# A two-layer LoRA residual kernel: W1's first rows turned by TensorE, two operand sums moved to adding DMAs, and G transposed by VectorE

## The chip, the cores and the metric

The kernel runs on one core of a Trainium2 chip. The metric is the device time of one execution in microseconds (us). The engines are TensorE (PE: matmuls; PEld: its weight loads), VectorE (DVE), ScalarE (ACT), GpSimd (POOL) and SyncE (SP). DMAs are issued from the queues of SP, ACT and POOL and move data on 16 DMA engines. Everything is float32.

## The reference

Two residual layers, each with a LoRA adapter that a token of the sequence selects:

```
# x: (8, 256, 1024); W0, W1: (1024, 1024); ranks 32 (layer 0) and 16 (layer 1)
x = x + x @ W0.T + 0.5 * (x @ A0[i0[b]]) @ B0.T
x = x + x @ W1.T + bias + 2 * (x @ A1[i1[b]]) @ B1[i1[b]]
```

Here `i0[b]` and `i1[b]` pick one of 3 and one of 24 (A1 and B1 hold 32) for each of the 8 sequences b.

## The kernel before, in words

**What is computed.** The kernel adds the identity to both weights and multiplies the two layers into one matrix, M = (W0 + I)^T (W1 + I)^T, then sends every sequence through M. The LoRA terms and the bias become a product of rank 64 per sequence that is added to the same sums. All large products are Strassen-Winograd products of 2x2 blocks (7 products and a handful of block sums), on two levels.

**Tiles.** `w0n` holds W0 + I, `w1T` holds the transposed W1 + I, `tw` its block sums; later the same space holds parts of M and of its sums. `m11`, `m21`, `m22` hold parts of M. `units` is 8 pieces of 128x1024: first W1 as it lands, later the sequences, landed and transposed. `s_all` is 4 pieces of 128x1024: the four sums s[0] to s[3] of the left operand that is being multiplied. `work` holds what was taken out of PSUM. The 8 PSUM banks are used in two sets of four: X and Y.

**Stages, as PE goes through them.**

- Start: 15 warm-up matmuls of `ident` by itself (L945), then 32 matmuls `first` (L978; 4 groups, 4 chunks k, 2 column halves) for the first block product. For each k, DVE transposes W1's first rows in 32x32 blocks (`turn_w1`, L227), adds the identity to their diagonal (L235) and to W0's (`diag_w0`, L182). SP loads W1's first half-block in four DMAs of 512-byte runs (`load_w1`, L168), then W0 (`load_w0`, L176), then the second half-block.
- The rest of the first block product as an inner Strassen product (`Second`, L530), then the LoRA products `prepare_up` (L723), `prepare_down` (L750) and `prepare_cross` (L764). `prepare_down` makes G^T = A1^T (W0 + I) for the 8 sequences, 128x1024, and ACT copies it to `gT`, a part of `work`.
- `product6` of the first group (L288, at 51.7 us), then `finish_down`: 8 PE transposes of `gT` (L778), copied from PSUM to `g1` by ACT (L779). `fill_down` (POOL, L817) later copies a sequence's 16 columns of `g1` into its `down`. Then the other block products (L288) and the last two row tiles of M as inner Strassen products (`Chain`, L530).
- Four pairs of sequences (`for q in range(B // 2)`). Each pair takes 7 inner Strassen products (`product`, L530), alternately into X and Y; in between come the down product of the next pair (`low_start`, L788, and `low_end`, L806) and the updates of rank 64 (L530 and L550).

**What sets the order.** The schedule is manual: each engine and each queue runs its instructions in the order in which the program writes them, and waits for semaphores. So the place of a line in the program is its place in its engine's queue.

**The lines that the steps below touch.** In the chain: `form` (L604 to L610) turns the seven products of a bank set into four blocks; the last one before the pairs, `form(chain.keep5, X, ...)`, comes after an ACT copy of slot 1 (L1135). `sums_1` to `sums_4` (L838, L841, L844, L847) make s[0] to s[3] of a pair on DVE, 128x1024 each; `z_sums` (L489) makes the four inner sums of one such operand. `Operand.sums` (L424 to L427) and `sums_rest` (L439) make the block sums of the right operand on DVE; `sums_dma` (L433 on ACT, L435 on POOL) makes three of them as ACT copies with a sign and POOL DMAs that add. `turn_x` (L240) transposes a landed sequence on DVE; `load_x` (L153) lands it in 8 SP DMAs of 64 KB. `add_up` (L515) adds a PSUM set to `work`, `keep` (L511, ACT) copies it there. `end` (L863) writes the last blocks.

In the first pair DVE makes, in this order: z of s[0], the sums of ops "t2", s[1] (L841), z of s[1], `diff`, chain t4, s[3] (L847), a rest sum (L439), z of s[3], s[2] (L844), the transposes of the next pair.

Of the kernel before, what the change touches and what calls it, by code (L numbers as in the profile page):

```python
# [10 lines left out]
ALU = mybir.AluOpType  # L11
# [9 lines left out]
P = 128  # L21
NH = 512
L0_SCALING = 16 / 32
L1_SCALING = 32 / 16
MLOW = 64
BIAS = 48
NWARM = 15
NV7 = 7
NWORK = 3
NUNIT = 8  # L30
NV = 2
NU = 2
NLOW = 4
NQ = NH // 2
NB = 4
# [6 lines left out]
def kernel(  # L42
# [120 lines left out]
    def load_w1(wq, h: int, i: int, lo: int = 0, hi: int = NR):  # L163

        rows = slice(h * NH + lo * SQ, h * NH + hi * SQ)
        for g in range(NG):
            cols = slice(i * NH + g * P, i * NH + (g + 1) * P)
            nc.sync.dma_start(  # L168
                wq[g * SQ : (g + 1) * SQ, lo:hi, :],
                w1[rows, cols].rearrange("(t q) c -> q t c", q=SQ),  # L170
            )

    def load_w0(k: int, i: int):
        cols = slice(i * NH, (i + 1) * NH)
        rows = w0[(k // NB) * NH : (k // NB + 1) * NH, cols]
        nc.sync.dma_start(  # L176
            w0n[:, k, cols], rows.rearrange("(p m) c -> p m c", m=NB)[:, k % NB, :]
        )

    def diag_w0(k: int):  # L180
        diag = w0n[:, k].rearrange("p (i q m) -> p i m q", i=2, m=NB)[:, k // NB, k % NB]
        nc.vector.tensor_tensor(diag, diag, ident, ALU.add)  # L182
# [66 lines left out]
    def new_bank():  # L249
        ring.append(ring.pop(0))  # L250
        return ring[-1]

    def low_bank():

        while ring[0] not in sets[0]:
            new_bank()
        return new_bank()

# [254 lines left out]
    def add_up(v, ps):  # L513
        for n in (3, 2, 1, 0):
            nc.vector.tensor_tensor(at_home(v, n), whole(ps, n), at_home(v, n), ALU.add)  # L515

    def low_region(ps):
        return ps[3][:, NQ:NH]
# [240 lines left out]
    def prepare_cross():  # L759
# [11 lines left out]
        nc.scalar.copy(cross.rearrange("p b r -> p (b r)"), pe)  # L771

    def finish_down():
        for h in range(NO):
            pt = (banks[7] if h else low_bank()).rearrange("p (m q) -> p m q", m=NB)
            chunks = gT[h].rearrange("p (j q c) -> p j c q", q=P, c=NX)
            for m in range(NB):
                nc.tensor.transpose(pt[:, m, :], chunks[:, m // NX, m % NX], ident)  # L778
            nc.scalar.copy(  # L779
                g1[:, NB * h : NB * (h + 1)].rearrange("p k b r -> p k (b r)"), pt  # L780
            )

# [33 lines left out]
    def fill_down(b: int):  # L816
        nc.gpsimd.tensor_copy(downs[b % NV][:, :, R0:RR], g1[:, :, b, :])  # L817

    class Pair:
# [26 lines left out]
        def sums_4(self):  # L846
            nc.vector.tensor_tensor(self.s[:, 3], self.x["12"], self.s[:, 1], ALU.subtract)  # L847

        def diff(self):
# [72 lines left out]
    with tc.manual_schedule(engines=ORDERED):  # L922
# [3 lines left out]
        wq[0, 0] = new_w1(0, 0)  # L926
        for n in range(2):
            load_w1(wq[0, 0], 0, 0, n * mid, (n + 1) * mid)
            if n == 0:
                for k in range(NB):  # L930
                    load_w0(k, 0)
        wq[0, 1] = new_w1(0, 1)
# [9 lines left out]

        for n in range(NWARM):
            bank, i = banks[4 + n // 4], n % 4
            nc.tensor.matmul(  # L945
                bank[:, i * P : (i + 1) * P],
                ident,
                ident,
                start=(i == 0),
                stop=True,  # L950
                skip_group_check=True,
            )
        raw0, raw1 = load_indices(idx0, 0), load_indices(idx1, 1)
# [22 lines left out]
        def first(g, k: int, n: int):  # L976
# [8 lines left out]
            )  # L985

        for k in range(NB):
            turn_w1(wq[0, 0], 0, k, 0, mid)
            diag_w0(k)
            for g in w_groups:  # L990
                first(g, k, 0)
# [61 lines left out]
        bias_rows(0)  # L1053
        load_up(0)
        for i, which in enumerate(("21", "22")):
            raws[which] = load_x(1, i, 6 + i)
# [10 lines left out]
        one.product6()  # L1067
        finish_down()
        seconds[1].form()
# [42 lines left out]
        for which in ("21", "22"):  # L1112
# [4 lines left out]
        chain.product(Y, "s4", "22", False)  # L1117
        ops["22"].sums_dma()
        ops["11"].sums_rest()
        add_up(chain.m12, Y)  # L1120
# [9 lines left out]
            low=(  # L1130
                lambda: low_start(0, pair.x, low_pl),
                lambda: low_end(0, low_pl),
            ),
        )
        nc.scalar.copy(chain.keep5[:, SLOT[1] * NQ : (SLOT[1] + 1) * NQ], slot(X, 1))  # L1135
        form(chain.keep5, X, chain.block(m21))
# [3 lines left out]
        ops["t3"].sums_dma()  # L1140
        z_sums(pair.sq(0), z_early[1])
        ops["t2"].sums()
        pair.sums_2()
        pending = []
# [7 lines left out]
        for q in range(B // 2):  # L1152
# [33 lines left out]
            if early:  # L1186
                chain.sums_m("t4")
                pair.sums_4()

# [9 lines left out]
            z_sums(pair.sq(3), pair.z[3])  # L1199
            if early:  # L1200
                pair.sums_3()
            if more:
# [40 lines left out]
            if not more:  # L1243
# [13 lines left out]
                low=(  # L1257
                    lambda: low_start(q + 1, following.x, pl7),
                    lambda: low_end(q + 1, pl7),
                ),  # L1260
            )
            nc.scalar.copy(kept2[:, SLOT[1] * NQ : (SLOT[1] + 1) * NQ], slot(X, 1))
            form(kept1)
# [53 lines left out]
```

## Time and profile before

| | us |
|---|---|
| median of three runs (329.24 to 329.58) | 329.51 |
| the profiled execution, its own time | 328.95 |
| its span in the trace | 327.2 |
| PE busy | 320.3 |
| DVE busy | 258.1 |
| ACT, POOL busy | 58.0, 65.6 |
| first L978 matmul starts | 7.13 |
| last matmul's chain ends, the tail follows | 323.9 |

The difference of 1.75 us between the profiled execution's time and its span lies outside what the trace records. In the lines of the profile, "x30" counts records; a float32 matmul of this kernel leaves two records, so 15 warm-up matmuls are x30 and 32 `first` matmuls are x64. In the timeline a line begins with start and length of a merged group; its bracket gives the idle time of the engine before it and what ended it. In the chain and wait views, "A <- B" reads: A waited for B. The `MATMUL` ends are modelled and overlap, so distances between starts are what counts. No PE wait is longer than 1.5 us, and between 32 and 130 us the trace shows none.

### The profile page before, as it was taken

The numbers are of one execution on the slowest core, as the hardware profiler recorded it, in microseconds if no ns is written. First come the engines' busy times: TensorE is split into PE (matmuls) and PEld (weight loads), VectorE is DVE, ScalarE is ACT, GpSimd is POOL, SyncE is SP. The second block draws the span as 40 slices with busy tenths as digits, with TensorE's granted clock in tenths as the row PEclk, the third lists the DMA queues.
The fourth block names the chain that finished last, engine by engine and source line by source line (L and its number), as shares of the span: only waits on it lengthen the run. The fifth ranks groups of instructions, "written<-read, shape, count | busy, mean of one in ns | idle before, by whom it ended". The sixth has DMA issues, their size and how long they took to land.

```text
span 327.2 us, 4443 instructions
## 1 busy us (share of the span) xinstructions
PE 320.3 (98%) x1506; PEld 248.8 (76%) x1506; DVE 258.1 (79%) x494; ACT 58.0 (18%) x124; POOL 65.6 (20%) x105
## 2 busy tenths in 40 slices
PE   8999999999999999999899999999999999999996
PEld 8888435444588878788678888877888887888884
DVE  5889997489899969999998775985774985622965
ACT  1042216010224222440001240001231001222000
POOL 6063303535212312641013000010100000000000
PEclk9999999999999999999999999999999999999999
DMA  7999945983066960993446510246510111100113
GB/s 207 207 253 197 291 90 79 191 145 59 8 91 121 183 100 11 146 170 60 118 114 160 148 27 0 79 131 178 145 34 0 64 66 64 64 2 1 64 66 128
DMA packets 64654, 34.85 MB, mean 107 GB/s; under 512 B 45252, under 2 KB 59188, under 8 KB 64632
## 3 DMA queue, kind: packets, MB, share of 16 engines
q1 hardware_dynamic: 56264, 20.61, 28.7%
q0 software_dynamic: 8368, 13.96, 20.4%
q8 instruction: 12, 0.20, 0.3%
q14 instruction: 10, 0.08, 0.1%
HBM read 19.02 MB, written 8.39 MB: 84 GB/s over the span
## 4 chain that ended last, share of the span: by engine, by line
PE 90%; DVE 6%; SPq 2%; DMA 1%; issue 1%; POOL 0%; DVEq 0%; POOLq 0%
PE bank L530 62%; PE bank L288 11%; PE bank L788 4%; PE bank L750 4%; PE bank L978 4%; PE bank L945 2%; DVE work L515 1%; SPq L153 1%; PE bank L723 1%; DVE units L240 1%; DMA down<-in_L_cond_lora_A_dram 1%; PE bank L550 1%; DVE w1T L489 1%; PE bank L806 1%; DVE m L489 0%
## 5 line engine op out<-in xcount | busy, mean ns | idle before, releaser
L515 DVE TENSOR_TENSOR work<-bank,work 128x512 f32<-128x512 f32 (+1 forms) x56 | 32.7, 619 | 20.7 <-PE bank L530 20.7
L511 ACT COPY work<-bank 128x512 f32<-128x512 f32 (+1 forms) x60 | 27.6, 547 | 67.9 <-PE bank L530 63.0
L916 POOL DMA_DIRECT2D out_dram<-work x12 | 8.9, 741 | 112.5 <-DVE work L610 109.0
L530 PE MATMUL bank<-w0n,w1T 128*128 128x256 f32 x104 | 24.1, 379 | 0.0
L530 PE MATMUL bank<-w1T,s_all 128*128 128x256 f32 x88 | 22.3, 380 | 0.7 <-DVE s_all L841 0.7
L240 DVE STREAM_TRANSPOSE units<-units 128x512 f32<-128x512 f32 x32 | 20.2, 684 | 2.9 <-DMA units<-in_x_dram 2.8
L530 PEld LDWEIGHTS bank<-w0n,w1T 128*128 128x128 f32 x104 | 19.8, 190 | 2.7
L530 PE MATMUL bank<-w0n,m 128*128 128x256 f32 x88 | 20.9, 380 | 0.0
L227 DVE STREAM_TRANSPOSE w1T<-units 128x512 f32<-128x512 f32 (+1 forms) x20 | 17.4, 914 | 4.1 <-DMA units<-in_L_cond_W_dram 4.0
L530 PEld LDWEIGHTS bank<-w1T,s_all 128*128 128x128 f32 x88 | 16.6, 190 | 3.2 <-issue 1.0
L530 PEld LDWEIGHTS bank<-w0n,m 128*128 128x128 f32 x88 | 16.6, 190 | 2.6 <-issue 0.4
L796 ACT ACTIVATE a<-bank,shift,scale 128x256 f32<-128x256 f32 x4 | 2.3, 564 | 89.5 <-PE bank L788 89.5
L530 PE MATMUL bank<-tw,m 128*128 128x256 f32 x68 | 17.4, 381 | 0.0
L530 PE MATMUL bank<-tw,s_all 128*128 128x256 f32 x64 | 16.1, 379 | 0.0
L530 PE MATMUL bank<-m,units 128*128 128x256 f32 x64 | 15.1, 379 | 0.0
L788 PE MATMUL bank<-units,down 128*64 128x256 f32 x128 | 14.7, 382 | 0.0
L530 PEld LDWEIGHTS bank<-tw,m 128*128 128x128 f32 x68 | 12.8, 190 | 2.1 <-issue 0.4
L530 PE MATMUL bank<-w0n,s_all 128*128 128x256 f32 x56 | 14.4, 379 | 0.0
L288 PE MATMUL bank<-tw,s_all 128*128 128x512 f32 x32 | 14.3, 595 | 0.0
L750 PE MATMUL bank<-w0n,a 128*128 128x512 f32 x32 | 14.3, 599 | 0.0
L978 PE MATMUL bank<-w1T,w0n 128*128 128x256 f32 x64 | 14.1, 381 | 0.0
L288 PE MATMUL bank<-w1T,s_all 128*128 128x512 f32 x32 | 14.1, 592 | 0.0
(258 smaller groups left out, 656.2 us busy)
## 6 DMA issues: line engine op xcount, KB each, us to landing
units<-in_x_dram SPq DMA_DIRECT2D x128, 64.0 KB, 2.6
out_dram<-work POOLq DMA_DIRECT2D x12, 512.0 KB, 3.4
w0n<-in_L_cond_W_dram SPq DMA_DIRECT2D x16, 256.0 KB, 7.0
units<-in_L_cond_W_dram SPq DMA_DIRECT2D x12, 256.0 KB, 8.3
out_dram<-work SPq DMA_DIRECT2D x3, 512.0 KB, 2.8
units<-in_L_cond_W_dram SPq DMA_DIRECT2D x8, 128.0 KB, 4.0
down<-in_L_cond_lora_A_dram SPq DMA_DIRECT2D x32, 32.0 KB, 2.3
w1T<-m POOLq DMA_DIRECT2D x4, 256.0 KB, 4.9
```

Source lines behind the costliest of these rows:

```text
L153: nc.sync.dma_start(xq[g * SQ : (g + 1) * SQ, :, n, :], x[b, :, first : first + SQ * NX].rearrange("(t q) c -> q t c", q=SQ),)
L227: nc.vector.transpose(w1T[:, k, cols].rearrange("p (t q) -> p t q", q=SQ), wq[:, lo:hi].rearrange("p t (q m) -> p m t q", m=NB)[:, k % NB],)
L240: nc.vector.transpose(xT[:, NX * j : NX * (j + 1), :].rearrange("p c (t q) -> p c t q", q=SQ), xq[:, :, j, :].rearrange("p t (q c) -> p c ...
L288: nc.tensor.matmul(pm, a[:, k, :], b(k), start=first and k == 0, stop=(k == NB - 1), skip_group_check=not first,)
L511: nc.scalar.copy(at_home(v, n), whole(ps, n))
L515: nc.vector.tensor_tensor(at_home(v, n), whole(ps, n), at_home(v, n), ALU.add)
L530: nc.tensor.matmul(slot(ps, i) if dst is None else dst, lhs, rhs, start=BANK[i][0] not in started, stop=stop, skip_group_check=True,)
L750: nc.tensor.matmul(pm, a1[:, k].rearrange("p b r -> p (b r)"), w0n[:, k, h * NH : (h + 1) * NH], start=(k == 0), stop=(k == NK - 1),)
L788: nc.tensor.matmul(pl[n * MLOW : (n + 1) * MLOW, :], downs[n][:, k, :], x_b[f"{n + 1}{k // NB + 1}"][:, k % NB, :], start=(k == 0), stop=( ...
L916: eng.dma_start(out[b, :, h * NH : (h + 1) * NH].rearrange("(j p) d -> p j d", p=P), ob[:, 0:D].rearrange("p (j d) -> p j d", d=NH),)
L945: nc.tensor.matmul(bank[:, i * P : (i + 1) * P], ident, ident, start=(i == 0), stop=True, skip_group_check=True,)
L978: nc.tensor.matmul(g.p1[:, cols], g.a[0][:, k, :], w1T[:, k, cols], start=False, stop=(k == NB - 1), skip_group_check=True,)
```

## The change

Five edits.

1. **Start.** W1's first 256 rows (columns 0 to 511) land in natural order in `units[:, 0]`, as two DMAs of 256 KB with 2 KB runs, one issued by SP and one by ACT (in place of four SP DMAs). After 6 warm-up matmuls PE transposes them in 8 matmuls of 128x128 into two banks, then runs 3 more warm-ups. ACT and DVE copy a bank each into `w1T`; DVE adds the four diagonals in one instruction. The four DVE transposes and four diagonal adds of the first half go.
2. **G.** `finish_down` no longer uses PE and ACT. `turn_down`, ahead of `product6`, transposes `gT` in 32x32 blocks with four DVE instructions into a free part of `m21`; 16 SP DMAs of 32 KB put the blocks in place in `g1`, whose layout is now (pair, k, r). They stand in SP's queue after `load_up(0)` and ahead of the 16 loads of the first pair's second sequence. `fill_down` reads the new layout.
3. **s[2] and s[3] of the first pair** leave DVE: ACT writes the negated operand into `s_all`, a POOL DMA of 512 KB adds the other one (`sums_dma` of `Pair`).
4. **Order on DVE.** `sums_2` and the z of s[0] move from behind the chain's last `form` and block sums to ahead of that `form`.
5. **`keep_v1`.** The ACT copy of slot 1 moves from behind the whole product to ahead of `low_start`, in the chain and in the three pairs that have a next one.

The core of the diff (the removed `low_bank` and the removed calls of `pair.sums_2`, `sums_3`, `sums_4`, `finish_down` and the two L1135/L1262 copies are left out):

```diff
-NWARM = 15
+NWARM = 6
+    def keep_v1(v, ps):
+        nc.scalar.copy(v[:, SLOT[1] * NQ : (SLOT[1] + 1) * NQ], slot(ps, 1))
...
+    def turn_down():
+        for h in range(NO):
+            for j in range(2):
+                k = 4 * h + NX * j
+                nc.vector.transpose(
+                    g_squares[:, :, k : k + NX, :].rearrange("p g c r -> p c g r"),
+                    gT[h][:, j * NQ : (j + 1) * NQ].rearrange("p (g q c) -> p c g q", q=SQ, c=NX),
+                )
     def finish_down():
-        for h in range(NO):
-            pt = (banks[7] if h else low_bank()).rearrange("p (m q) -> p m q", m=NB)
-            chunks = gT[h].rearrange("p (j q c) -> p j c q", q=P, c=NX)
-            for m in range(NB):
-                nc.tensor.transpose(pt[:, m, :], chunks[:, m // NX, m % NX], ident)
-            nc.scalar.copy(
-                g1[:, NB * h : NB * (h + 1)].rearrange("p k b r -> p k (b r)"), pt
-            )
+        for g in range(NG):
+            for both in range(NG):
+                nc.sync.dma_start(
+                    g_all[g * SQ : (g + 1) * SQ, both], g_squares[both * SQ : (both + 1) * SQ, g]
+                )
...
+        def sums_dma(self, i: int, which: str, other):
+            nc.scalar.mul(self.s[:, i], other, -1.0)
+            nc.gpsimd.dma_start(self.s[:, i], self.x[which], accum_op=ALU.add)
...
+        w1_rows = units[:, 0].rearrange("p (t c) -> p t c", t=2)
+        for t, engine in enumerate((nc.sync, nc.scalar)):
+            engine.dma_start(w1_rows[:, t], w1[t * P : (t + 1) * P, 0:NH])
+        for k in range(NB):
+            load_w0(k, 0)
+        load_w1(wq[0, 0], 0, 0, mid, NR)
...
+        warm_up(0, NWARM)
+        w1_turned = [banks[4 + t].rearrange("p (m q) -> p m q", m=NB) for t in range(2)]
+        for t in range(2):
+            for m in range(NB):
+                rows = w1_rows[:, t].rearrange("p (q m) -> p m q", m=NB)[:, m]
+                nc.tensor.matmul(w1_turned[t][:, m, :], rows, ident, ..., is_transpose=True, ...)
+        warm_up(4, 7)
...
+        nc.scalar.copy(w1T[:, 0:NB, P : 2 * P], w1_turned[1])
+        nc.vector.tensor_copy(w1T[:, 0:NB, 0:P], w1_turned[0])
         for k in range(NB):
-            turn_w1(wq[0, 0], 0, k, 0, mid)
             diag_w0(k)
+            if k == 0:
+                part = w1T[0:MLOW, 0, 0:1]
+                diag = bass.AP(part.tensor, part.offset, [part.ap[0], [D + 1, NB], [NB, MLOW]])
+                same = ident[0:MLOW, 0:MLOW].unsqueeze(1).to_broadcast([MLOW, NB, MLOW])
+                nc.vector.tensor_tensor(diag, diag, same, ALU.add)
...
         load_up(0)
+        turn_down()
+        finish_down()
...
         ops["22"].sums_dma()
+        pair.sums_dma(2, "11", pair.x["21"])
...
-                lambda: low_start(0, pair.x, low_pl),
+                lambda: (keep_v1(chain.keep5, X), low_start(0, pair.x, low_pl)),
...
+        pair.sums_2()
+        z_sums(pair.sq(0), z_early[1])
+        pair.sums_dma(3, "12", pair.s[:, 1])
         form(chain.keep5, X, chain.block(m21))
```

## The prediction

> **What bounds the kernel now.** I read the page's busy times and chain first, then PE's waits, then the timelines around each wait. The page says that PE is the bound nearly everywhere:
>
> ```profile
> PE 320.3 (98%) x1506; PEld 248.8 (76%) x1506; DVE 258.1 (79%) x494; ACT 58.0 (18%) x124; POOL 65.6 (20%) x105
> ...
> PE 90%; DVE 6%; SPq 2%; DMA 1%; issue 1%; POOL 0%; DVEq 0%; POOLq 0%
> ```
>
> PE is idle for 327.2 - 320.3 = 6.9 us. The list of PE's waits places them; the rest (about 3.3 us) is the tail after the last matmul, which the change doesn't touch:
>
> ```profile
> PE bank L945 <- POOL ident masks.py:199: 1.5, 1, 1.5
> PE bank L530 <- DVE w0n L439: 1.0, 1, 1.0
> PE bank L530 <- DVE s_all L841: 0.7, 1, 0.7
> PE bank L550 <- DVE work L515: 0.5, 1, 0.5
> ```
>
> The last three are waits for DVE, all in the first pair of sequences (0.65 us at 134.5, 0.98 at 157.7, 0.45 at 162.5 in PE's timeline), 2.08 us in all. The table by stage shows why: from 130 to 160 DVE is the full engine (29.60 of 30 us) and PE the one with gaps:
>
> ```profile
> 130.00:160.00 30.00, 28.37 (x137) 23.86 (x136) 29.60 (x55) 6.80 (x14) 11.27 (x13) 1.00 0.72 123
> ```
>
> So time is won only by taking work off PE, by relieving DVE ahead of those three waits, or by an earlier start. The change tries all three.
>
> **1. G without PE.** PE's timeline:
>
> ```profile
> 51.74 3.70 PE L288 MATMUL bank<-tw,s_all 128*128 128x512 f32 x8
> 55.28 1.11 PE L778 MATMUL bank<-ident,work 128*128 128x128 f32 x8
> 56.23 3.60 PE L288 MATMUL bank<-tw,s_all 128*128 128x512 f32 x8
> ```
>
> The eight transposes take 56.23 - 55.28 = 0.95 us between products with no gap on either side: **-0.95**. What must not be late in their place: `product7` needs s[2] (DVE, done at 48.2) and a bank long free; it can start at once. The added four DVE transposes read 128x256 each: between 0.32 (half of L240's 128x512 row, 0.62 start to start, same stride of 2) and 0.64 (L227's 128x256, stride 4), so 1.3 to 2.6 us. They stand at 53.6, where DVE idles 1.96 us before L308, and 1.18 and 2.74 us more before the next two PSUM reads, each of which waits for PE; DVE is back on PE's heels by 63. No matmul before 70 us reads what that delay touches (the next, `other.product6` at 69.96, needs s[1] at 68.7, made after those idles). The ACT copies of 1.07 us go; nobody queued on them. The 16 DMAs of 32 KB issue on SP from about 58.2, at 0.5 to 0.68 us each (L219's and L153's rows: 10.84 us for 16), until 66 to 69. Queued behind them are 16 loads of x (10.8 us, then to 80 plus 2.6 to land) that DVE reads at 103.0: 20 us spare. `g1` is read by POOL at 78.7, and the part of `m21` is written by DVE at 77.0: 6 us spare. Cost 0; if that cover were gone, 1 us of delay would first eat these 6.
>
> **2. The first pair.** All in before's clock. DVE's and ACT's rows:
>
> ```profile
> 121.59 0.42 DVE L604 TENSOR_TENSOR work<-bank,work 128x256 f32<-128x256 f32 x1 [2.22 <-ACT work L1135]
> ...
> 133.11 1.22 DVE L841 TENSOR_TENSOR s_all<-s_all,units 128x1024 f32<-128x1024 f32 x1
> 137.27 1.21 DVE L847 TENSOR_TENSOR s_all<-units,s_all 128x1024 f32<-128x1024 f32 x1
> ...
> 140.47 1.22 DVE L844 TENSOR_TENSOR s_all<-units 128x1024 f32<-128x1024 f32 x1
> ```
>
> DVE idles 2.22 us before L604. s[1] (133.11 to 134.37, 1.26) and z of s[0] (129.11 to 130.58, 1.47) move there: 2.73 us of work into a hole of 2.22. `form` so starts at 122.1, not 121.6, but everything behind the moved work is 2.2 earlier. With `keep_v1` early, `form` no longer waits for ACT. s[3] gone is 1.14 more (137.27 to 138.41), s[2] gone 1.31 (140.47 to 141.78). So DVE leads by 2.2 from 132, by 3.4 from 137, by 4.7 from the transposes on (137.1 instead of 141.8).
>
> Is that enough for the three waits? s[1] is ready at 120.6 instead of 134.3: wait one (0.65) goes. Next in line there are the sums of "t2", first read 1.8 us into that product; they end at 131.9, its start is 133.8. Then the lead is cut: x "22" loads into the unit that PE reads until 133.8, its 8 issues end at 138.2 and land 2.6 later, 140.8; DVE now wants it at 140.1. Lead left: about 4.0. Waits two and three need 0.65 + 0.98 and 2.08: both go, with 2 us over. **-2.08**. Until then DVE must not be late for PE's product of s[0], the tightest one: "t1"'s t4 ends at 127.0, PE reads it at 129.4.
>
> What makes s[2] and s[3] now: ACT negates 128x1024 (twice the 0.57 of an L433 row of 128x512: 1.1 us), for s[3] after L807 at 121.3, so until 122.4; ACT is idle there till 128 except L433's 1.7 us, whose DMA waits for DVE until 128.6 anyway. Then a POOL issue of about 1.2 us and a landing: the adding rows of 256 KB take 3.8 to 4.2 us, so 512 KB take between 4.2 (if latency is all) and 8.4 (if size is all): 127 to 131. DVE needs s[3] at 139.01 - 3.4 = 135.6, PE at 140. I take 8.4; cost 0, cover 4.6 us. "t3"'s adding DMAs queue behind on POOL, wait for DVE till 128.6, and are needed at 139.5, with 137.1 by before's rows.
>
> The other `keep_v1` moves shorten DVE idles (7.3 us before L604 over three pairs) for which PE never waited: 0.
>
> **3. The start.** PE's and DVE's rows:
>
> ```profile
> 1.51 5.79 PE L945 MATMUL bank<-ident 128*128 128x128 f32 x30 [1.51 <-POOL ident masks.py:199]
> 7.13 14.09 PE L978 MATMUL bank<-w1T,w0n 128*128 128x256 f32 x64
> ...
> 5.74 0.64 DVE L227 STREAM_TRANSPOSE w1T<-units 128x256 f32<-128x256 f32 x1 [2.56 <-DMA units<-in_L_cond_W_dram]
> ```
>
> By the landings in the trace W1's first 512 KB are there at 5.6 in before; its four DMAs land 0.7 us apart (128 KB each, 512-byte runs), W0's of 256 KB with 2 KB runs 0.7 to 0.9 apart, so twice the rate. The first DMA lands at 3.6, about 2.9 plus 0.7. So the two new DMAs, side by side, land at about 2.9 + 2 x 0.7 = 4.3, W0's first at 5.0. Warm-up records start 0.213 apart until about 6.1 and 0.107 apart afterwards (30 records from 1.51 to 7.1 fit only so), though the granted clock reads 1.00 throughout. Hence:
>
> - 6 warm-ups, 12 x 0.213: PE busy until 4.07; then 8 transposes, one record each (L778: x8 for 8), 8 x 0.213 = 1.7: until 6.0.
> - ACT's copy of the second bank, 0.59 (L302, 128x512): 6.6. DVE meanwhile copies the first and adds W0's diagonal.
> - The joint diagonal add, 256 elements, 0.4 (L489's 128x256): 7.0. L978 starts at about **7.05**; before 7.13. The three warm-ups end by 6.65 at the fast spacing.
>
> The 0.17 us that PEld later waits for L235 goes too, as DVE comes to the second half with less behind it; that half lands at about 9.7, is turned by 13.8, read at 13.9. Start: 0.08 + 0.17 = **-0.25**, with bounds of -0.7 (landing at 3.9) and +0.7 (the ACT queue's DMA late by 1 us).
>
> **The sum.** 328.95 - 0.95 - 2.08 - 0.25 = 325.67 for an execution like the profiled one. The median of the runs shown lies 0.56 above that execution, so I forecast **326.2**.
>
> **Rivals.**
>
> *PE stays slow for longer (25%).* Matmuls took twice as long until 4.6 us after the first one. If transposes don't count towards that, only the three warm-ups at 6.0 restart it: fast from 10.6. Warm-ups then end at 7.3, and L978 runs at half speed for 3.3 us, losing 0.25 + 1.65 = 1.9: **328.1**. For: 8 of 17 early matmuls are now transposes. Against: PE has no gap, and nothing in this trace separates kinds. The Trainium skill's page "TensorE: Matmul & The Clock Gate" speaks for this rival: Part 4 says of transpose mode that it "doesn't count as PE-busy the same way", and Part 1 that the clock stays halved until a window of about 3.4 us was busy; the doubling at 6.1 agrees with Part 1, and no row here tests Part 4. By that rule the sum would be this rival's.
>
> *DVE's lead is lost again (12%).* If x "22" or "t3"'s last adding DMA comes 2 to 4 us later because 1 MB of adding DMAs shares the engines, waits two and three stay in part: +0.7 to +1.4, **327.2**. For: DMA engines are 0.72 busy in that stage. Against: 2 us spare in the sum above.
>
> *The adding DMA of s[3] is the new bound (5%): slower.* Place: z of s[3], then PE's product of s[3]. Up to 137.9 only DVE's spare lead goes; after that each us is lost, and past 141.9 more than the whole gain: 19.5 us after the negation at 122.4, against 8.4 by the rows. Price if it takes 21 us: about **331**.
>
> *Nothing is gained (2%)*: another wait takes the place of all three and the start loses 1 us, 329.5. That the change doesn't do what it says: the order of instructions has PE without the eight transposes and DVE without the two sums, so I give it none.
>
> The forecast has 56%: 325.7 to 327.1 with the start's bounds. **Range 325.3 to 328.5**: it adds the spread of the runs shown (0.3) and takes in the slow-clock and lost-lead cases. Faster by over 0.2%, 0.66 us, which is about what a measurement of this kernel can tell from no change: 56 + 25 + 11 = 92%; within: 3%; slower: 5%.
>
> **What would show it.** PE's waits: L841, L439 and L515 gone from the list; no L778 row. L978's first start near 7.05 and an end near 20.8; record spacing of 0.107 in the warm-ups after the transposes (0.213 there means rival one). DVE idle in front of PSUM reads at 145 to 160 where it had none. A DVE wait of more than 2 us for a DMA on `s_all` means rival three. A transpose record above 0.25 us, or PE waiting for ACT or DVE at 6 to 8 us by more than 0.5, would break my start.

## The result and the profile after

| | before | after |
|---|---|---|
| median (7 executions each, on the same chip) | 329.58 us (329.24 to 330.12) | 325.99 us (325.34 to 327.99) |
| the profiled execution, its own time | 328.95 | 325.99 |
| its span | 327.2 | 323.9 |
| PE busy | 320.3 | 318.3 |
| DVE busy | 258.1 | 254.8 |

The ratio is 0.9907, with a 95% interval of 0.9891 to 0.9923: 3.1 us faster (2.5 to 3.6). The medians lie 3.59 apart; two of after's seven executions, 327.85 and 327.99, lie well above the others and pull the ratio. The forecast was 326.2. In the profiled pair the kernel gains 2.96 us, and the forecast had 3.28 there.

The page of the kernel after, its busy times and its chain that ended last, the lines that answer to the prediction's first fence:

```profile
PE 318.3 (98%) x1494; PEld 247.3 (76%) x1494; DVE 254.8 (79%) x490; ACT 59.9 (18%) x125; POOL 68.9 (21%) x107
...
PE 98%; DVE 0%; ACT 0%; POOL 0%; issue 0%; POOLq 0%
```

PE was 90% of the chain and DVE 6%; now PE is 98% of it and DVE 0%. PE's list of waits after says the same:

```profile
PE bank L963 <- POOL ident masks.py:199: 1.5, 1, 1.5
PE bank L1012 <- DVE w1T L1030: 0.6, 1, 0.6
```

The three waits for DVE (L841, L439, L515 in the numbers of before) are gone, and a new one stands in front of the first real matmul. In the table by stage, the row that had 28.37 us of PE before has 30.00 after, with DVE as full as it was (columns: PE, PEld, DVE, ACT, POOL, the clock, the DMA share, GB/s):

```profile
130.00:160.00 30.00, 30.00 (x151) 25.68 (x151) 29.66 (x60) 7.52 (x16) 12.73 (x14) 1.00 0.76 134
```

**Where the time went.** I compare the starts of the same matmuls in the two traces (in the numbers of after; a minus is earlier):

| PE reaches | before | after | difference | this stretch |
|---|---|---|---|---|
| first L1012 | 7.13 | 7.73 | +0.60 | start |
| `product6` (first L282) | 51.74 | 52.47 | +0.73 | start: +0.73 in all |
| the low product of the first pair (L797) | 114.85 | 114.63 | -0.22 | G: -0.95 |
| past the first wait | 134.48 | 133.45 | -1.03 | -0.81 |
| past the second wait | 157.68 | 155.43 | -2.25 | -1.22 |
| the next pair's low product, by the chain | 168.98 | 165.49 | -3.49 | -1.24 |
| last matmul's chain ends | 323.97 | 320.47 | -3.50 | 0 |

In this pair of traces the start lost 0.73, G won 0.95 and the first pair won 3.27. The tail behind the last matmul is 0.2 longer, and what lies outside the span 0.34 longer (2.09 against 1.75), which makes -2.96.

Two of the three stretches hardly vary. From `product6` to the low product it takes 63.1 us in every trace of the runs below with the old G and 62.15 or 62.16 with the new one; from there to the next low product 54.04 to 54.06 with none of edits 3 to 5, and 50.78 to 50.90 with all three. The start does vary, and one pair of traces doesn't give its price: `product6` begins at 51.74 to 52.76 (mean 52.24) in the seven traces with the old start (before, `e2_g_only`, `e3_pair_only`, `e4_old_start`, `e6_s2_only`, `e7_order_only`, `e12_old_start_again`), and at 52.09 to 52.62 (mean 52.39) in the three of the new one (after, `e1_start_only`, `e11_after_again`). The trace of before has the earliest start of all, so some 0.5 of the 0.73 lies in that trace and not in the edit. The tail, on the other hand, is 3.4 us in every trace with the new start and 3.2 to 3.3 in every one with the old.

### The profile page after: what moved, and what is told of

Its sections match the earlier page's. It is cut to its first block, busy times and chain, and to the rows that moved or that the text cites. A ratio compares the mean times of both kernels' runs of the same rounds, so it can differ in the third digit from the quotient of the medians.

```text
span 323.9 us, 4429 instructions
## 1 busy us (share of the span) xinstructions
PE 318.3 (98%) x1494; PEld 247.3 (76%) x1494; DVE 254.8 (79%) x490; ACT 59.9 (18%) x125; POOL 68.9 (21%) x107
## 4 chain that ended last, share of the span: by engine, by line
PE 98%; DVE 0%; ACT 0%; POOL 0%; issue 0%; POOLq 0%
PE bank L527 71%; PE bank L282 11%; PE bank L797 4%; PE bank L747 4%; PE bank L1012 4%; PE bank L720 1%; PE bank L963 1%; PE bank L977 1%; PE bank L815 1%; DVE w1T L1030 0%; ACT w1T L1021 0%; PE bank L761 0%; PE bank L547 0%; DVE work L885 0%; POOL ident masks.py:199 0%
## 5 line engine op out<-in xcount | busy, mean ns | idle before, releaser
L527 PE MATMUL bank<-w0n,w1T 128*128 128x256 f32 x104 | 24.1, 379 | 0.0
L527 PE MATMUL bank<-w1T,s_all 128*128 128x256 f32 x88 | 22.3, 379 | 0.0
L527 PEld LDWEIGHTS bank<-w0n,w1T 128*128 128x128 f32 x104 | 19.8, 190 | 2.7
L527 PE MATMUL bank<-w0n,m 128*128 128x256 f32 x88 | 20.9, 380 | 0.0
L227 DVE STREAM_TRANSPOSE w1T<-units 128x512 f32<-128x512 f32 (+1 forms) x16 | 14.9, 989 | 5.2 <-DMA units<-in_L_cond_W_dram 5.1
L527 PEld LDWEIGHTS bank<-w0n,m 128*128 128x128 f32 x88 | 16.6, 190 | 2.6 <-issue 0.4
L527 PEld LDWEIGHTS bank<-w1T,s_all 128*128 128x128 f32 x88 | 16.7, 190 | 2.3
L527 PE MATMUL bank<-tw,m 128*128 128x256 f32 x68 | 17.4, 381 | 0.0
L527 PE MATMUL bank<-tw,s_all 128*128 128x256 f32 x64 | 16.1, 379 | 0.0
L527 PE MATMUL bank<-m,units 128*128 128x256 f32 x64 | 15.1, 379 | 0.0
L797 PE MATMUL bank<-units,down 128*64 128x256 f32 x128 | 14.7, 382 | 0.0
L1012 PE MATMUL bank<-w1T,w0n 128*128 128x256 f32 x64 | 14.1, 381 | 0.6 <-DVE w1T L1030 0.6
L527 PEld LDWEIGHTS bank<-tw,m 128*128 128x128 f32 x68 | 12.8, 190 | 2.1 <-issue 0.4
L527 PE MATMUL bank<-w0n,s_all 128*128 128x256 f32 x56 | 14.4, 379 | 0.0
L282 PE MATMUL bank<-tw,s_all 128*128 128x512 f32 x32 | 14.2, 595 | 0.0
L282 PE MATMUL bank<-w1T,s_all 128*128 128x512 f32 x32 | 14.1, 592 | 0.0
L1012 PEld LDWEIGHTS bank<-w1T,w0n 128*128 128x128 f32 x64 | 12.5, 196 | 2.0 <-DVE w1T L1030 0.8
```

Of the source, the lines that this page charges most:

```text
L227: nc.vector.transpose(w1T[:, k, cols].rearrange("p (t q) -> p t q", q=SQ), wq[:, lo:hi].rearrange("p t (q m) -> p m t q", m=NB)[:, k % NB],)
L282: nc.tensor.matmul(pm, a[:, k, :], b(k), start=first and k == 0, stop=(k == NB - 1), skip_group_check=not first,)
L527: nc.tensor.matmul(slot(ps, i) if dst is None else dst, lhs, rhs, start=BANK[i][0] not in started, stop=stop, skip_group_check=True,)
L797: nc.tensor.matmul(pl[n * MLOW : (n + 1) * MLOW, :], downs[n][:, k, :], x_b[f"{n + 1}{k // NB + 1}"][:, k % NB, :], start=(k == 0), stop=( ...
L1012: nc.tensor.matmul(g.p1[:, cols], g.a[0][:, k, :], w1T[:, k, cols], start=False, stop=(k == NB - 1), skip_group_check=True,)
```

## The start after, line by line

The timeline of after, 0 to 24 us (start, length, engine and line; the bracket is the idle time before it):

```profile
1.51 2.93 PE L963 MATMUL bank<-ident 128*128 128x128 f32 x12 [1.51 <-POOL ident masks.py:199]
...
4.44 1.98 PE L977 MATMUL bank<-ident,units 128*128 128x128 f32 x8
...
6.21 0.90 PE L963 MATMUL bank<-ident 128*128 128x128 f32 x6
6.46 0.59 ACT L1021 COPY w1T<-bank 128x512 f32<-128x512 f32 x1 [3.62 <-PE bank L977]
7.07 0.60 DVE L1030 TENSOR_TENSOR w1T<-w1T,ident 64x256 f32<-64x256 f32 x1 [0.45 <-ACT w1T L1021]
...
7.73 14.09 PE L1012 MATMUL bank<-w1T,w0n 128*128 128x256 f32 x64 [0.62 <-DVE w1T L1030]
...
11.74 0.65 DVE L227 STREAM_TRANSPOSE w1T<-units 128x256 f32<-128x256 f32 x1 [1.49 <-DMA units<-in_L_cond_W_dram]
```

The data landed at 4.44, close to the 4.3 of the prediction. What it missed is the way from there to the first real matmul: the copy starts at 6.46 and not 6.0, since the eighth transpose starts only at 6.00 (its modelled end is 6.42); the copy ends at 7.05; the joint diagonal add took 0.60 and not 0.4. Each is small; with the later landing they make 0.68. And the last line: DVE waited 1.49 us for the second half of W1, which landed at 11.74 and not 9.7 (in before its first transpose started at 11.39). So the 0.17 us of the later wait were not to be had either. In another profiled execution of the same kernel (`e11_after_again`) the first real matmul did start at 7.13, and the next product still only at 21.73 (21.66 here), with a wait of 0.26 for the diagonal add of the second half: then that half is what is late. This is no price of the edit: the old start has it too. PE's timeline of `e4_old_start`, which has 15 warm-ups and W1's first rows turned by DVE:

```profile
7.69 8.40 PE L994 MATMUL bank<-w1T,w0n 128*128 128x256 f32 x38
16.36 5.89 PE L994 MATMUL bank<-w1T,w0n 128*128 128x256 f32 x26 [0.27 <-DVE w1T L235]
22.09 2.11 PE L527 MATMUL bank<-w1T,w0n 128*128 128x256 f32 x9
```

Over the traces named above, the first real matmul starts at 7.13 to 7.72 with the old start and at 7.13 to 7.73 with the new one, and DVE's first transpose of the second half at 11.39 to 12.42 and 11.52 to 12.07.

## The experiments

Medians stand beside a median of the kernel before from the same chip: 329.53 for the first four, 329.68 for the next four, 329.47 for three, 329.55 for the last. Differences in us are worked out from the ratio, its interval in brackets. In the expectations, A is the theory that the three stretches are worth what the table above reads (start +0.6, G -0.95, first pair -3.1), and B that the prediction's own terms hold.

**The start alone** (before with edit 1):

```diff
-NWARM = 15
+NWARM = 6
...
-            load_w1(wq[0, 0], 0, 0, n * mid, (n + 1) * mid)
+            engine.dma_start(w1_rows[:, t], w1[t * P : (t + 1) * P, 0:NH])
...
+                nc.tensor.matmul(w1_turned[t][:, m, :], rows, ident, ..., is_transpose=True, ...)
...
+        warm_up(4, 7)
...
```

> The kernel before with the new start alone (W1's first rows turned by TensorE). Theory A, from the traces of before and after: the first real matmul begins at 7.73 instead of 7.13 us and nothing of that is won back, so +0.6 to +0.7 us against before (about 330.2), and single executions scatter by up to 2 us upward, as those of after do (325.3 to 328.0). Rival B, the prediction's own term: -0.25 us, with the scatter of before (329.2 to 330.1).

Measured: 329.84, ratio 1.0019 [1.0004, 1.0035], +0.6 (0.1 to 1.2). Its first real matmul starts at 7.49, and its list of PE's waits has the new wait beside the three old ones (here the second, third and last line are before's):

```profile
PE bank L530 <- DVE w0n L439: 1.0, 1, 1.0
PE bank L996 <- DVE w1T L1014: 0.7, 1, 0.7
PE bank L530 <- DVE s_all L841: 0.7, 1, 0.7
PE bank L550 <- DVE work L515: 0.5, 1, 0.5
```

The edit costs time, and the -0.25 lies outside the interval. How much it costs is less sure: three of the twelve executions, 331.23 to 331.50, lie well above the others and pull the ratio, and the medians are only 0.3 apart. In this run's trace `product6` starts at 52.09, 0.35 later than in before's, and inside what the old start shows.

**G alone** (before with edit 2):

```diff
-                nc.tensor.transpose(pt[:, m, :], chunks[:, m // NX, m % NX], ident)
...
+                nc.vector.transpose(...)
...
+                nc.sync.dma_start(
+                    g_all[g * SQ : (g + 1) * SQ, both], g_squares[both * SQ : (both + 1) * SQ, g]
+                )
...
```

> The kernel before with G transposed by VectorE and put in place by DMAs, nothing else. Theory A: PE loses the eight transposes and waits for nothing in their place, -0.95 us, about 328.6; the first pair's three waits then stay as they are. Rival B: the DVE work added there or the SP queue makes PE wait somewhere before the first pair, or the waits for DVE in the first pair grow by what was won, so 0 to -0.3 us.

Measured: 328.69, ratio 0.9965 [0.9951, 0.9979], -1.15 (-1.6 to -0.7). The three waits for DVE stand unchanged at 1.0, 0.7 and 0.5. The 0.95 that was read off PE's timeline is what the edit gives.

**The first pair alone** (before with edits 3, 4 and 5: the adding DMAs, the order, `keep_v1`):

```diff
+        pair.sums_dma(2, "11", pair.x["21"])
...
+        pair.sums_2()
+        z_sums(pair.sq(0), z_early[1])
+        pair.sums_dma(3, "12", pair.s[:, 1])
         form(chain.keep5, X, chain.block(m21))
...
```

> The kernel before with the edits of the first pair alone (s[2] and s[3] by ScalarE and adding DMAs, the new order on VectorE, the early copy of slot 1). Theory A: each of PE's three waits cost more than the list of waits shows (0.81, 1.14 and 1.15 us by the distances between matmul starts), so -3.1 us, about 326.5. Rival B: they cost what the list shows, -2.08 us, about 327.5, and the rest of after's gain comes from elsewhere.

Measured: 326.42, ratio 0.9904 [0.9888, 0.9919], -3.2 (-3.7 to -2.7). None of the three waits is left. The prediction's -2.08 lies outside the interval: B falls.

**All but the start** (after with before's start):

```diff
-NWARM = 6
+NWARM = 15
...
-            engine.dma_start(w1_rows[:, t], w1[t * P : (t + 1) * P, 0:NH])
+            load_w1(wq[0, 0], 0, 0, n * mid, (n + 1) * mid)
...
-        warm_up(4, 7)
...
+            turn_w1(wq[0, 0], 0, k, 0, mid)
```

> The changed kernel with the old start (15 warm-ups, W1's first rows by VectorE). Theory A: the sum of the two parts that gain, -0.95 - 3.1 = -4.05 us against before, about 325.5, that is 0.6 us faster than the changed kernel's quick executions and without the ones near 328. Rival B, the start earns 0.25 us: slower than the changed kernel by that much.

Measured: 325.44, ratio 0.9879 [0.9857, 0.9901], -4.0 (-4.7 to -3.3). That agrees with G and the pair together (-1.15 - 3.16 = -4.3), and it is 0.55 below the median of after, which comes from another set of runs.

**Do transposes count?** Rival one of the prediction, tested by itself: before, with its 15 warm-up matmuls replaced by 30 transposes of `ident`, one record each.

```diff
-        for n in range(NWARM):
-            bank, i = banks[4 + n // 4], n % 4
-            nc.tensor.matmul(bank, ident, ident, start=(i == 0), stop=True, ...)
+        for n in range(2 * NWARM):
+            bank, i = banks[4 + n % 16 // 4], n % 4
+            nc.tensor.matmul(bank, ident, ident, start=..., stop=True, is_transpose=True, ...)
```

> The kernel before with its 15 warm-up matmuls (two records each) replaced by 30 transposes of the same matrix (one record each), so that TensorE is as busy for as long. Theory C, transposes do not count towards the faster spacing: the 30 records start 0.213 us apart to the end, until about 7.9 us, the first real matmuls start 0.427 us apart per record for some 4.6 us more, so about +0.8 + 2.3 = +3 us, 332 to 333. Rival D, they count: the spacing drops to 0.107 between 5 and 8 us as in before, same time as before within 0.3 us; the scatter of the new start then has another cause.

Measured: 329.63, ratio 0.9995 [0.9979, 1.0011]: the time of before. PE's table by stage of this kernel, PE's busy time and in brackets the records (the clock reads 1.00 in all rows):

```profile
3.50:5.20 1.70, 1.70 (x10) 1.00 1.06 229
5.20:6.90 1.70, 1.67 (x14) 1.00 0.93 290
```

and of before:

```profile
3.50:5.20 1.70, 1.70 (x10) 1.00 1.10 222
5.20:6.90 1.70, 1.70 (x13) 1.00 1.00 333
```

At the first spacing of 0.213, a stretch of 1.7 us holds 8 starts (the count of 10 has records that reach in from outside); the 14 in the second show the faster spacing, although PE had run nothing but transposes. By the starts of single records the spacing changes from 0.21 to 0.11 at 5.40. Rival one falls.

**s[2] alone** by ACT and an adding DMA, in before's order:

```diff
+        pair.sums_dma(2, "11", pair.x["21"])
...
-            if early:
-                pair.sums_3()
```

> The kernel before with s[2] alone made by ScalarE and an adding DMA; s[3] and the order on VectorE are as before. Theory A, PE's three waits (0.81, 1.14, 1.15 us by starts) are one lag of VectorE, and each us that VectorE is freed of ahead of them is won up to 3.1 us: VectorE is freed of 1.31 us after the first wait, so -1.3 us, about 328.2; first wait still there, second gone, about 1 us of the third left. Rival E, what is freed is lost again where VectorE waits for the landing of the next pair's x: 0 to -0.3 us.

Measured: 328.29, ratio 0.9959 [0.9939, 0.9978], -1.35 (-2.0 to -0.7). PE's waits in the first pair:

```profile
PE bank L530 <- DVE s_all L841: 0.6, 1, 0.6
PE bank L550 <- DVE work L515: 0.4, 1, 0.4
```

The work of 1.31 us leaves DVE behind the first wait and ahead of the second, so the first stays and the second goes. By starts, from the low product to the next, the pair takes 52.73 us against 54.06: -1.33.

**The order alone** (before with edits 4 and 5):

```diff
-        nc.scalar.copy(chain.keep5[:, SLOT[1] * NQ : (SLOT[1] + 1) * NQ], slot(X, 1))
+        pair.sums_2()
+        z_sums(pair.sq(0), z_early[1])
...
-        z_sums(pair.sq(0), z_early[1])
...
-        pair.sums_2()
```

> The kernel before with the new order on VectorE and the early copy of slot 1, but s[2] and s[3] on VectorE as before. Theory A: 2.2 us of idle VectorE time are filled ahead of the first wait, so first and second wait go, about 0.9 us of the third is left: -2.2 us, about 327.3. Rival E: only the first wait goes, -0.8 us, about 328.7.

Measured: 327.58, ratio 0.9941 [0.9922, 0.9959], -1.95 (-2.6 to -1.35). Of the three waits only the last is left (two new ones of 0.3 us stand in this trace's start):

```profile
PE bank L553 <- DVE work L515: 0.4, 1, 0.4
```

By starts the pair takes 51.87 us, -2.19. A lead of 2.2 us, the idle time in front of `form` that the moved work fills, is worth about that. So in this pair what DVE is relieved of ahead of the waits comes back one for one (1.33 for 1.31, 2.19 for 2.2), until the stalls, 3.1 us, are used up (3.27 for 4.7).

**Ordinary matmuls for the transposes** (after, without the transpose flag):

```diff
-                    is_transpose=True,
```

> The changed kernel with W1's first rows turned by ordinary matmuls with the identity (two records each) instead of transposes. Theory C: TensorE is then warmed without a break, the spacing drops to 0.107 by 8 us in every execution, so the executions near 328 are gone; the longer turning (up to 8 more records of 0.107 to 0.213) costs 0.85 to 1.7 us at the start, so 326.6 to 327.4 with a spread of about 0.5. Rival D: the same cost, and the spread of 2.6 us stays.

Measured: 328.18, ratio 0.9947 [0.993, 0.9965], -1.75 (-2.3 to -1.15), so 1.3 above after by the two ratios and 2.2 by the medians. The step leaves 16 records in place of 8 and takes 4.00 us in place of 1.98; the first real matmul starts at 9.70, 1.97 later than in after. `product6` starts at 54.30, 1.83 later, and the profiled execution takes 327.80, 1.81 more: the length of this step is on the path. The expectation of 0.85 to 1.7 for the step was too low, as these records stood 0.24 us apart ((8.22 - 4.38) / 16) on average, with no faster end. The nine executions lie within 0.93 us, nearer to C's 0.5 than to D's 2.6.

**No gap ahead of the first real matmul** (after, with six warm-ups behind the transposes in place of three):

```diff
-        warm_up(4, 7)
+        warm_up(4, 8)
+        warm_up(4, 6)
```

> The changed kernel with six instead of three warm-up matmuls behind the transposes, so that TensorE has no gap, or hardly one, before its first real matmul. Theory F: the executions near 328 are those in which the gap of 0.6 us before that matmul puts off the faster spacing by another stretch of some 3.4 us, 1.8 us lost; with the gap filled there are none, all lie within 1.0 us (six warm-ups at the slow spacing end at 8.8 instead of 7.73), median 325.7 to 326.4. Rival G, the spread has nothing to do with the start: some executions stay 1.5 us or more above the median.

**After, again, beside it:** the kernel after, unchanged.

> The changed kernel itself once more, as the control on the same chip: most executions 325.3 to 326.0, some near 328 by either theory.

**All but the start, again, beside both:** the kernel of `e4_old_start`, unchanged.

> The changed kernel with the old start once more, beside the changed kernel on the same chip. Theory A: 0.5 to 0.6 us faster than the changed kernel's quick executions (325.4 against 325.9), and faster by more in the median if the changed kernel's executions near 328 are frequent. Rival B: no faster than the changed kernel.

Measured on the same chip:

| kernel | median, executions | ratio to before |
|---|---|---|
| six warm-ups behind the transposes | 325.72 (325.52 to 326.53, 5) | 0.9885 [0.9861, 0.991] |
| after | 326.07 (325.03 to 327.41, 6) | 0.989 [0.9863, 0.9917] |
| after with before's start | 325.79 (325.38 to 326.33, 5) | 0.9888 [0.9865, 0.9911] |

The three can't be told apart here. With six warm-ups the wait for L1030 leaves PE's list, but the first real matmul starts at 7.50, between after's 7.73 and the 7.13 of `e11_after_again`, so the gap is only filled. Theory F took the executions of after that lie 1.5 to 2 us above the others (327.85 and 327.99 of seven, 327.41 of six) for the price of that gap. None came in the five executions without a gap. But none came either in the nine of `e8_turn_by_matmul`, whose gap is 0.64 us; one of the six of `e4_old_start` (327.25) and three of the twelve of `e7_order_only` (1.1 to 1.5 above its median), which have no such gap, lie nearly as far up, and so do single executions of before (332.05 of 29, 331.48 of 11). None of those executions was profiled. F is not shown.

**Six warm-ups and then nothing** (before, with its first data as late as ever). It leaves nine warm-up matmuls out and spreads the six over the same four banks; some sums that start in columns which those no longer write come out differently, and every later instruction is the same. (With `NWARM` alone changed, `e10_six_warmups`, there is no time on record.)

```diff
-NWARM = 15
+NWARM = 6
...
-            bank, i = banks[4 + n // 4], n % 4
+            bank, i = banks[4 + n % 4], n // 4
```

> The kernel before with six warm-up matmuls ahead of the first piece of W1 instead of fifteen, so that TensorE has nothing to do for some 2 us more before the transposes. Theory F (the faster spacing of matmuls comes some time after TensorE has been kept busy without a break, so that an idle stretch in front of the real work puts it off): the doubling of the matmul rate, seen at about 6.1 us in the kernel before, comes 3.4 us or more after the end of the idle stretch; the first real matmuls run at half rate for 3.4 to 6.8 us and lose half of that, +1.7 to +3.4: 331.2 to 333 us. Rival G (the faster spacing depends only on the time since the first matmul, and not on what lies between): the time of the kernel before within 0.5 us, 329.0 to 330.1 us.

Measured: 331.27, ratio 1.0058 [1.0041, 1.0074], +1.9 (1.35 to 2.4). PE stood idle for 2.75 us, and the first real matmul started at 7.19, as in before (7.13). PE's table by stage of this kernel, busy time and records:

```profile
7.20:8.70 1.50, 1.50 (x4) 1.00 1.11 298
8.70:10.20 1.50, 1.50 (x5) 1.00 1.21 182
10.20:11.70 1.50, 1.50 (x8) 1.00 1.23 200
```

and of before:

```profile
7.20:8.70 1.50, 1.50 (x8) 1.00 0.92 279
8.70:10.20 1.50, 1.50 (x8) 1.00 1.22 229
10.20:11.70 1.50, 1.50 (x8) 1.00 1.24 208
```

Half as many records until 10.2, then as many. PE is "busy" in all of them, and the clock column reads 1.00. From the first real matmul to the next product it takes 22.67 - 7.19 = 15.48 us against 21.07 - 7.13 = 13.94, 1.54 more. So an idle stretch of 2.75 us, ahead of the doubling, puts the doubling off to some 3 us after the work goes on (record starts 0.41 to 0.43 apart until 10.32, 0.21 from there: 3.1); the rival, by which only the time since the first matmul counts, falls. The Trainium skill's page "TensorE: Matmul & The Clock Gate", Part 1, has the clock halved until a window of about 3.4 us was busy. The 3.1 us of this run lie just under that.

## Why the prediction was right, and where its terms were not

The median fell 0.2 us from the forecast, and that it came so close is luck. The mechanisms of G and of the first pair held; the start earned nothing. In the profiled pair the errors nearly cancel: the sum had 1.2 us too little in the first pair, against 1.0 too much at the start and 0.5 behind the last matmul and outside the span, where it had nothing. The 0.56 added to get from the profiled execution to the median has to do with the same start: before's profiled execution, 328.95, is faster than all its seven others, while after's is its median.

- **G, -0.95: right.** The trace gives -0.95, the run alone -1.15 (-1.6 to -0.7), and -0.96 in its trace. The covers held. The next fence is DVE's and PE's part of the timeline of after around it:

```profile
52.47 7.13 PE L282 MATMUL bank<-tw,s_all 128*128 128x512 f32 x16
...
55.44 1.42 DVE L780 STREAM_TRANSPOSE m<-work 128x256 f32<-128x256 f32 x4
```

PE goes through both products without a break, and the four transposes took 1.42 us, the low end of 1.3 to 2.6. The SP queue of after:

```profile
60.37 12.81 SPq L788 DMA_DIRECT2D g<-m  x16
73.22 3.11 SPq L153 DMA_DIRECT2D units<-in_x_dram  x6
```

The 16 DMAs were issued one every 0.80 us, not 0.5 to 0.68 (one record lasts 0.59 in the median, 1.29 at most), and ended at 73.2, not 66 to 69. The 20 us of cover behind them took it: DVE doesn't wait for x there. The tighter cover was the 6 us ahead of `g1` and `m21`: the last of these DMAs was issued at 72.6 and they landed 1.8 to 4.6 us after issue, so at most 2.4 us were left before DVE's write at 76.80. Neither DVE nor POOL (77.61) waits there.

- **The first pair, -2.08: right mechanism, wrong size.** All three waits went, as forecast. But the wait list had them too small. PE's timeline of before, around the second and third:

```profile
157.68 1.13 PE L530 MATMUL bank<-w0n,units 128*128 128x256 f32 x4 [0.98 <-DVE w0n L439]
...
161.33 0.70 PE L530 MATMUL bank<-up,diff 64*128 64x256 f32 x2
162.48 0.48 PE L550 MATMUL bank<-w1T,diff 64*128 64x256 f32 x1 [0.45 <-DVE work L515]
...
164.40 1.13 PE L530 MATMUL bank<-m,w1T 128*128 128x256 f32 x4
```

and of after:

```profile
153.70 1.89 PE L527 MATMUL bank<-m,units 128*128 128x256 f32 x8
155.43 1.03 PE L527 MATMUL bank<-w0n,units 128*128 128x256 f32 x4
...
158.98 0.48 PE L527 MATMUL bank<-up,diff 64*128 64x256 f32 x1
158.98 0.48 PE L547 MATMUL bank<-w1T,diff 64*128 64x256 f32 x1
```

A bracket counts from the modelled end of the matmul before, which lies beyond the start that its successor could have had. In after L527's and L547's records start together at 158.98; in before L550's came 162.48 - 161.33 = 1.15 after L530's, and the list called that 0.45. Reading starts in before alone, the same update takes 164.40 - 161.33 = 3.07 where an undisturbed one (145.01 to 146.94) takes 1.93: 1.14 lost. In the same way the first wait cost 0.81 (0.65 listed) and the second 1.14 (0.98): 3.1 in all (the other 0.17 of the table's 3.27 lies in steps of 0.1 or less between them). The text ahead of the prediction says that distances between starts are what counts; this step did not use them. The run of the pair alone confirms the size (-3.7 to -2.7).

- **The lead of DVE: right, with room.** The transposes start at 137.68; 137.1 was forecast, 141.78 it was before. That lead of 4.1 exceeds the three stalls, so no wait is left; with less freed, waits stay (`e6_s2_only`, `e7_order_only`). One sign that the prediction named didn't come: DVE has no idle time in front of its PSUM reads at 145 to 160 and is busy for 29.66 of the 30 us, since PE itself comes up to 3.5 us earlier and so takes up most of the lead. `keep_v1` of the other pairs gave 0, as forecast: behind the first pair the difference stays at -3.5.

- **The adding DMAs (rival three): cover held.** POOL's part of the timeline of after:

```profile
116.73 1.21 POOL L862 DMA_DIRECT2D s_all<-units  x1
122.46 0.86 POOL L862 DMA_DIRECT2D s_all<-units  x1 [4.51 <-ACT s_all L861]
```

They landed 4.5 and 6.0 us after issue, nearer to the end of the bounds (4.2 to 8.4) at which latency decides. s[3] was there by 128.5, and DVE read it at 136.1. (The 137.9 of that rival doesn't follow from its own terms, 135.6 plus the 2 us over being 137.6; nothing here hangs on it.)

- **The start, -0.25: wrong.** The run alone excludes it: +0.6 (0.1 to 1.2) by the ratio, +0.3 by the medians. Three steps of the text failed. The chain behind the landing was too short (6.0, 6.6, 7.0 in the text; 6.46, 7.05, 7.67 in the trace), and the sign that the prediction named for it, a PE wait of more than 0.5 us at 6 to 8 us, is there with 0.62. The second half landed at 11.5 to 12.1 and not 9.7. And the old start was taken from one trace that happened to be early: its 7.13 and its `product6` at 51.74 are the earliest of seven. Against the mean of those seven the three traces of the new start reach `product6` 0.15 later, which their scatter of 1 us can't tell from nothing. The bounds given, -0.7 to +0.7, take the cost in, for another reason than the one stated. That the change would be better without it is likely but not settled: `e4_old_start` is 0.55 below after's median, and `e12_old_start_again` can't be told from after.

- **The tail and what lies outside the span, put at nothing: 0.5 us.** The prediction said that the change doesn't touch the tail; it is 0.1 to 0.2 us longer in each trace with the new start. Outside the span lie 2.0 to 2.15 us in the executions of after, 1.91 to 1.99 in those of `e4_old_start` and `e12_old_start_again`, and 1.69 to 1.82 in those of before, so the new start has a part in both. The kernels with the new start are the only ones here that issue a DMA from ACT's queue; whether that is the cause is not shown.

- **Rival one (25%): refuted, and its price is real.** The trace of after shows the first real block at full rate, 14.09 us as in before. The warm-ups behind the transposes stand 0.11 us apart, not the 0.213 that the prediction named as this rival's sign. Transposes count (`e5_warm_by_transposes`). For fp32 transposes of 128x128 the measurement speaks against Part 4 of the Trainium skill's page "TensorE: Matmul & The Clock Gate", which the prediction quoted. What does put the full rate off is idleness: 2.75 us of it cost 1.54 us in the trace, close to the 1.65 that the rival was given.

## What to carry to other kernels

Where an engine that feeds PE is full, as DVE is here, expect the work taken off it ahead of PE's waits to come back one for one until the stalls are used up, as it did in three runs of this kernel; size those stalls by the distances between the starts of matmuls, against an undisturbed repeat of the same group, not by the list of waits. A faster landing is worth nothing until the whole chain from the landing to the first matmul is added up, the leaving of PE, the copy and the last add included, and the next piece of data as well. Before a price is read from the starts of two traces, look how far the same start varies between traces: here by 1 us, more than the term that was to be won. Keep TensorE busy with anything, transposes too, until the real work comes.

## What the runs showed of the hardware that was not expected

- Three stalls listed as 0.65, 0.98 and 0.45 us cost 0.81, 1.14 and 1.14 by starts.
- 30 fp32 transposes bring the doubled record rate as 15 matmuls do (0.9995 [0.9979, 1.0011]); 2.75 us of idle PE ahead of it put it off to some 3 us after the idle stretch, with the clock column at 1.00 throughout.
- The doubling came at different times in different profiled executions, between 4.9 us (`e11_after_again`) and 7.3 (G alone, the pair alone, all but the start), where matmuls or transposes run from 1.51 us on in each, in the first with a pause of under 0.6 us ahead of 4.59. The Trainium skill's page "TensorE: Matmul & The Clock Gate", Part 1, says that the window runs freely, so that the moment varies from run to run; with 3.4 us from that page the doubling would come between 4.9 and 8.3 (an estimate: one to two windows after 1.51). These times lie within, the earliest at the edge. What lifts some executions by 1.5 to 2 us is open.
- An fp32 transpose of 128x128 leaves one record where an ordinary matmul by the identity leaves two. Eight took 1.98 us, and 1.23 in `e11_after_again`, where the doubling came at the second of them; eight matmuls took 4.00.
- DMAs of 32 KB within SBUF were issued every 0.80 us on SP, and an adding one of 512 KB landed 4.5 to 6.0 us after its issue.
